# A four-layer graph network on one core: quartered matrix loads in the second pass, a longer planned store, 22 instead of 24 early sums, and a shorter patience beside the LSTM

## The chip, the core and the metric

The kernel runs on one core of one Trainium2 chip. The metric is the device time of one execution in microseconds (us). "About 0.5%" below means a difference of 6.6 us.

## The reference, cut to what matters

There are 32 graphs of 512 nodes with 128 features. `adj` is a symmetric 512 x 512 matrix of zeros and ones with a unit diagonal for each graph. Four layers follow each other, each of the form `x = x + layer(relu(layernorm(x)), adj)`.

```python
# layer 0: masked attention
q, k, v = relu(h Wq + bq), relu(h Wk + bk), relu(h Wv + bv)
x = x + softmax(where(adj, clip(q k^T), -9e15)) v
# layer 1: normalized sums over the neighbours, times the LSTM's output
A = d^-1/2 (adj + I) d^-1/2
lw = lstm(conv(last 128 nodes of h))        # 128 steps in sequence, all 32 graphs at once
x = x + sigmoid((A h) lw)
# layer 2: four chained layers, each with row- and column-normalized sums over adj
# layer 3
x = x + prelu(adj (h W) + bias)
```

The LSTM of layer 1 needs only the last 128 nodes of every graph after layer 0. Its 128 steps depend on each other.

## The kernel before, in words

All work is written as operations of a planner (`Plan`, L522) and is put into a fixed order for each engine when the kernel is built. An operation names its engine (or two that could do it), a cost in us, a rank, and what it reads and writes. The planner places the operation that can start earliest by its own costs, lower ranks first. On the chip every engine then runs its list in that order and waits where the data aren't there yet. So an operation whose data come later than planned holds up everything behind it on its engine.

There are three stages.

* **First pass** (`pass_1`, L1115; ranks from 10,000): for each of the 32 graphs the keys, values and queries, and the attention of the last 128 nodes, then the convolution that feeds the LSTM. Keys, queries' input and values are stored to DRAM (L1156, L1157).
* **LSTM with the second pass beside it** (`lstm`, L1209, ranks 0 to 127; `pass_2`, L1278, ranks from 20,000). A step on TensorE (L1223) is 16 small matmuls in 128 x 32 tiles of the array: 8 for the step itself and 8 that prepare a later one. Then come tanh on ScalarE (L1249, L1261), the cell on VectorE (L1255, L1256), tanh on ScalarE (L1263), and the output with its transpose on VectorE (L1267, L1268), which the next step reads. Between two steps TensorE does work of the second pass: attention of the other 384 nodes (queries L1303, scores L1312, weighted values L1321, all in 128 x 32 tiles), and the sums of layer 1 over the neighbours (`sums_of_1`, L1370, with `aggregate`, L1402; its matmuls are L1406, eight of 128 x 512 on the full array for one graph). The last four graphs' second pass has ranks in the third stage.
* **The rest** (`rest`, L1420, ranks from 30,000): for each graph the product with the LSTM's output, layer 2 and layer 3, in an order of turns that begins with graphs 26 and 27 (`FIRST`).

`EARLY` is the set of graphs whose layer 1 sums are made in the second pass, beside the LSTM: there the whole matrix is loaded (L1291, 1 MB), squared into the form that the sums use while its degrees are accumulated (`squares`, L1355, four ScalarE instructions at L1360), the sums are made, stored (L1348) and loaded again in the third stage. For these graphs layer 1's normalized input overwrites x in place (`place=xc` in `ln_apply`, L1049: L1054 on VectorE, L1057 on ScalarE), so it waits until the store of x to DRAM (L1332) has read it. For other graphs three quarters of each row are enough in the second pass (L1295, 768 KB), and the sums are made in the third stage. Both kinds load the whole matrix in the third stage (L1428), except the two of `FIRST`.

Three planner numbers matter here. `gap` is the time from a transfer's issue slot to its landing, as planned: `LANDED` = 3.8 us for second-pass loads, and 2.0 us by default, which the store at L1332 has. `patience` is by how much an operation may run over the planned start of the next LSTM operation on its engine: 0.15 us for most, `PATIENCE` = 1.3 us for the eight-matmul sums of the second pass, which the planner takes to be 1.86 us long. The rule is in `Plan.run`:

```python
elif held is not None and s < held < s + o.engines[e][0] - o.patience:
    continue
```

SyncE issues nearly all transfers, in the order of its list, and waits at each for what that transfer needs.

Of the kernel before, what the change touches and what calls it, by code (L numbers as in the profile page):

```python
# [13 lines left out]
P = 128  # L14
# [744 lines left out]
def symmetric(ctx, tc, x, adj, weights, cols, rows, lstm_b, prelu_a, out, fail):  # L759
# [12 lines left out]
    nc = tc.nc  # L772
    B, N, D = x.shape
    NT = N // P
    T = P
    L = NT - 1
    NR = N - P
    MANY = 512 // (4 * B)
    LATE = 4
    FIRST = [B - LATE - 2 + k for k in range(2)]  # L780
    EARLY = range(24)
    FOLDS = (4, 7, 10, 13)
    MOVED = range(2, B - 2)
    TURN = 32
    T_STEP = 0.22
    SOON = 9_950.0
    LANDED = 3.8
    PATIENCE = 1.3
    plan_rest = 30_000
    assert D == P and N == 512  # L790

# [14 lines left out]
    def flat(ap):  # L806
        return ap.rearrange("p a b -> p (a b)")

    def f32(ap):
        return ap.bitcast(FP)  # L810
# [5 lines left out]
    def new(tag, shape, name, dtype=FP):  # L816
        return plan.cell(sb, tag, shape, dtype, name)
# [8 lines left out]
    def t_r(n):  # L826
        return max(0.112, n * 0.000455)
# [9 lines left out]
    def t_dma(kb):  # L837
        return 0.1 + kb / 315.0

    def PE(rank, t, fn, r=(), w=(), **k):  # L840
        return plan.op({"PE": (t, fn)}, rank, r, w, **k)

    def ACT(rank, t, fn, r=(), w=(), **k):
        return plan.op({"ACT": (t, fn)}, rank, r, w, **k)
# [7 lines left out]
    def DMA(rank, kb, fn, r=(), w=(), **k):  # L852
        return plan.op({"SP": (max(0.45, t_dma(kb)), fn)}, rank, r, w, gap=k.pop("gap", 2.0), **k)
# [6 lines left out]
    def evict(rank, n, dst, src, r, w, relu=False, scale=None):  # L860

        def act():
            nc.scalar.activation(dst(), src(), AF.Relu if relu else AF.Copy, **({} if scale is None else {"scale": scale}))

        def dve():
            if relu:
                nc.vector.tensor_scalar_max(dst(), src(), 0.0)
            elif scale is not None:
                nc.vector.tensor_scalar_mul(dst(), src(), scale)
            else:  # L870
                nc.vector.tensor_copy(dst(), src())

        slow = 0.0 if scale is None else 0.2
        return plan.op({"ACT": (t_act(n) + slow, act), "DVE": (t_dve(n), dve)}, rank, r, w)
# [157 lines left out]
    def ln_stats(rank, xc, tiles, name, at=0):  # L1032

        st = new("st", (P, NT, 6), f"f_st_{name}")
        mv = new("mv", (P, NT, 2), f"f_mv_{name}")
        for t in tiles:
            DVE(rank, 0.19, lambda t=t: nc.vector.bn_stats(st.t[:, t, :], xc.t[:, t - at, :]), [(xc, t - at)], [(st, t)])
        for t in tiles:
            DVE(rank, 0.09, lambda t=t: nc.vector.bn_aggr(mv.t[:, t, :], st.t[:, t, :]), [(st, t)], [(mv, t)])
        return mv  # L1040
# [8 lines left out]
    def ln_apply(rank, xc, mean, rstd, shift, r, name, relu=False, place=None):  # L1049

        xn = place or new("xn", (P, NT, P), f"f_xn_{name}")
        for t in range(NT):
            def dve(t=t):
                nc.vector.tensor_scalar(xn.t[:, t, :], xc.t[:, t, :], mean(t), rstd(t), OP.subtract, OP.mult)  # L1054

            def act(t=t):
                nc.scalar.activation(xn.t[:, t, :], xc.t[:, t, :], AF.Relu, bias=shift(t), scale=rstd(t))  # L1057
            either = {"ACT": (t_act(P) + 0.13, act)}
            if not relu:
                either["DVE"] = (t_dve(P), dve)  # L1060
            plan.op(either, rank, [(xc, t)] + r, [(xn, t)])
        return xn
# [215 lines left out]
    def pass_2(b):  # L1278
        R = 20_000 + b * 10 if b < B - LATE else 30_000 + (b - B + LATE) * 10 + 15
        dkq, dv, dl, dx = kept[b]  # L1280
        early = b in EARLY
        whole = early or b in FIRST
        a = new("a" if whole else "ar", (P, NT, N if whole else NR), f"f_a_{b}")
# [3 lines left out]
        xc = new("x", (P, NT if whole else L, P), f"f_x2_{b}")  # L1287
        DMA(R, 192, lambda: nc.sync.dma_start(hT.t, dkq.t[:, N:]), [dkq], [hT], gap=LANDED)
        DMA(R, 256, lambda: nc.sync.dma_start(keys.t, dkq.t[:, :N]), [dkq], [keys], gap=LANDED)
        if whole:  # L1290
            DMA(R, 1024, lambda: nc.sync.dma_start(a.t, adj[b].rearrange("(t p) j -> p t j", p=P)), [], [a], gap=LANDED)  # L1291
            ar, deg = squares(R, b, a, "2")
            mask, rows_of = ar, lambda j: f32(ar.t[:, j, :NR])
        else:
            DMA(R, 768, lambda: nc.sync.dma_start(a.t, adj[b, :, :NR].rearrange("(t p) j -> p t j", p=P)), [], [a], gap=LANDED)  # L1295
            mask, rows_of = a, lambda j: a.t[:, j, :]
        DMA(R, 258, lambda: nc.sync.dma_start(v.t, dv.t), [dv], [v], gap=LANDED)
        DMA(R, 192, lambda: nc.sync.dma_start(xc.t[:, :L, :], x[b, :NR].rearrange("(t p) d -> p t d", p=P)), [],
# [30 lines left out]
        if whole and not early:  # L1329
            begun[b] = a, xc, ar, deg  # L1330
        else:
            DMA(R + 5, 192, lambda: nc.sync.dma_start(dx.t, xc.t[:, :L, :]), [(xc, t) for t in range(L)], [dx])  # L1332
        mv = ln_stats(R, xc, range(L), f"r{b}")
        l1 = lns[b]
        POOL(R, 0.15, lambda: nc.gpsimd.tensor_copy(ln1[:, b, 0, :L], mv.t[:, :L, 0]), [mv], [(l1, "mr")])
# [19 lines left out]
    def squares(rank, b, a, name):  # L1355

        ar = new("ar", (P, NT, N), f"f_ar{name}_{b}", FR)
        deg = new("dg", (P, NT), f"f_deg{name}_{b}")
        for t in range(NT):
            ACT(rank, 0.62, lambda t=t: nc.scalar.activation(ar.t[:, t, :], a.t[:, t, :], AF.Square,  # L1360
                                                             accum_out=deg.t[:, t : t + 1]), [a], [(ar, t), (deg, t)])
        return ar, deg

    def diagonal(rank, ar, op):
# [5 lines left out]
    def sums_of_1(rank, b, xc, ar, rs):  # L1370
# [4 lines left out]
        xs = ln_apply(rank, xc, lambda t: ln1[:, b, 0, t : t + 1], lambda t: rs.t[:, t : t + 1], lambda t: sh.t[:, t : t + 1],  # L1375
                      [l1, rs, sh], f"c{b}", place=xc if b in EARLY else None)
        xp = relu_parts(rank, xs, f"c{b}")
        pg = bank(f"f_pg_{b}")
        diagonal(rank, ar, OP.add)
        first = aggregate(rank, xp, ar, pg)  # L1380
        gT = xc if b in EARLY else new("gs", (P, N), f"f_gT_{b}")
        evict(rank, N, lambda: gT.t if b not in EARLY else flat(gT.t), lambda: pg.t, [pg], [gT])
        return gT, first
# [10 lines left out]
    def relu_parts(rank, xs, name):  # L1394

        parts = new("y", (P, NT, 2, P), f"f_xp_{name}", FR)
        ACT(rank, 0.52, lambda: nc.scalar.activation(parts.t[:, :, 0, :], xs.t, AF.Relu), [xs], [(parts, 0)])
        DVE(rank, t_dve(N), lambda: nc.vector.scalar_tensor_tensor(  # L1398
            parts.t[:, :, 1, :], xs.t, 0.0, f32(parts.t[:, :, 0, :]), OP.max, OP.subtract), [xs, (parts, 0)], [(parts, 1)])
        return parts  # L1400

    def aggregate(rank, parts, ar, pg):  # L1402

        def half(k):
            for j in range(NT):
                nc.tensor.matmul(pg.t, parts.t[:, j, k, :], ar.t[:, j, :], start=(k == 0 and j == 0),  # L1406
                                 stop=(k == 1 and j == NT - 1))

        def both():
            half(0)  # L1410
            half(1)
        if rank < plan_rest:
            last = PE(rank, 8 * t_r(N), both, [parts, ar], [pg])
            last.patience = PATIENCE
            return last
        for k in range(2):
            last = PE(rank, 4 * t_r(N), lambda k=k: half(k), [(parts, k), ar], [pg])
        return last

    def rest(b, turn, lw_after):  # L1420
        R = 30_000 + turn * 10
        dkq, dv, dl, dx = kept[b]
        if b in begun:
            a, xc, ar, deg = begun[b]
        else:
            a = new("a", (P, NT, N), f"f_a3_{b}")
            xc = new("x", (P, NT, P), f"f_x3_{b}")
            DMA(R, 1024, lambda: nc.sync.dma_start(a.t, adj[b].rearrange("(t p) j -> p t j", p=P)), [], [a])  # L1428
            DMA(R, 192, lambda: nc.sync.dma_start(xc.t[:, :L, :], dx.t), [dx], [(xc, t) for t in range(L)])
            DMA(R, 64, lambda: nc.sync.dma_start(xc.t[:, L, :], dl.t), [dl], [(xc, L)])  # L1430
            ar, deg = squares(R, b, a, "")
        dinv = new("dv", (P, TURN // NT, NT), f"f_dinv_{b}")
        l1 = lns[b]
        rs = None if b in EARLY else new("rs", (P, NT), f"f_rs_c{b}")

# [12 lines left out]

        if b in EARLY:
            gT, first = new("gs", (P, N), f"f_gT3_{b}"), None  # L1450
# [171 lines left out]
@with_exitstack  # L1622
def kernel(
    ctx: ExitStack,
    tc: tile.TileContext,
    x: bass.AP,
    adj: bass.AP,
    weights: bass.AP,
    cols: bass.AP,
    rows: bass.AP,  # L1630
    lstm_b: bass.AP,
    prelu_a: bass.AP,
    out: bass.AP,
):
    nc = tc.nc
    tensors = (x, adj, weights, cols, rows, lstm_b, prelu_a, out)
    flags = ctx.enter_context(tc.tile_pool(name="flags", bufs=1))
    fail = flags.tile([P, 1], mybir.dt.int32, name="fail")
    with ExitStack() as pools:
        failed = symmetric(pools, tc, *tensors, fail)  # L1640
    with tc.If(failed > 0, preferred_fallthrough_block=False), ExitStack() as pools:
        general(pools, tc, *tensors)
# [58 lines left out]
```

## Time and profile before

| what | value |
|---|---|
| three executions | 1314.0, 1319.26 and 1320.12 us, median 1319.26 |
| profiled execution: time, span | 1317.18 us, 1315.4 us |
| TensorE busy | 1275.1 us (97%) |
| VectorE, ScalarE, GpSimd busy | 992.6 us (75%), 833.2 us (63%), 392.4 us (30%) |
| HBM traffic | 138.16 MB read, 62.65 MB written |
| first LSTM matmul, last one | 184.4 us, 521.4 us from the span's start |

The profiled execution is 2.1 us under the median, and its span lies 1.8 us under its own time. TensorE's busy time counts a matmul until its modelled end, so that neighbours overlap; a stretch at 97% still has room. The program writes each matmul of the 32-bit kind once, and the trace shows it as two records where it is not the one-pass kind: four planned quarter matmuls (called a row below) are eight records.

### The profile page before, as it was taken

How to read it: one execution, taken by the hardware profiler on the slowest of the kernel's cores; microseconds unless marked ns; L12 is line 12 of the kernel's file. 1: busy time of each engine (PE TensorE's matmuls, PEld its weight loads, DVE VectorE, ACT ScalarE, POOL GpSimd, SP SyncE). 2: the span in 40 equal slices, each digit the busy share in tenths (PEclk: the TensorE clock that was granted, in tenths of full speed). 3: DMA queues.
4: the chain of work that ended last, by engine and by line, in shares of the span. 5: the costliest groups of instructions: out<-in, count | busy, mean ns of one | idle time of the engine just before them, and what ended most of it. 6: DMA issues, size and time to landing. Idle time of an engine off the chain costs nothing.

```text
span 1315.4 us, 32850 instructions
## 1 busy us (share of the span) xinstructions
PE 1275.1 (97%) x12097; PEld 974.1 (74%) x12098; DVE 992.6 (75%) x3286; ACT 833.2 (63%) x2095; POOL 392.4 (30%) x737
## 2 busy tenths in 40 slices
PE   8999999999899899999999999999999999999997
PEld 6888866666576666777777878778787787787774
DVE  7998877767788786977676767777676777787654
ACT  5666757667587565577566666666666675676423
POOL 4655532212242222443031322313222132242101
PEclk9999999999999899999999999999999999999999
DMA  8888888766777555999576677777777755673311
GB/s 264 257 277 279 274 272 254 250 214 205 225 243 243 151 165 163 216 213 207 130 158 159 155 156 163 164 158 152 154 164 161 165 120 90 151 170 72 49 33 35
DMA packets 300585, 234.50 MB, mean 178 GB/s; under 512 B 138240, under 2 KB 244480, under 8 KB 300416
## 3 DMA queue, kind: packets, MB, share of 16 engines
q1 hardware_dynamic: 283520, 215.54, 59.4%
q0 software_dynamic: 16896, 16.78, 8.1%
q8 instruction: 97, 1.59, 0.5%
q14 instruction: 72, 0.59, 0.1%
HBM read 138.16 MB, written 62.65 MB: 153 GB/s over the span
## 4 chain that ended last, share of the span: by engine, by line
PE 84%; DVE 6%; DMA 4%; ACT 3%; issue 2%; POOL 1%; SPq 0%; ACTq 0%; DVEq 0%; POOLq 0%
PE f_pa L1406 17%; PE f_py L1510 15%; PE f_pa L1521 14%; PE f_pg L1406 9%; PE f_s L1312 4%; PE f_z L1223 4%; PE f_po L1321 4%; PE f_p L1562 2%; PE f_pol L1173 2%; PE f_pk L1130 2%; PE f_pv L1146 2%; PE f_pl L1464 2%; PE f_sl L1163 2%; DMA f_a<-in_adj_dram 2%; PE f_pd L1198 1%
## 5 line engine op out<-in xcount | busy, mean ns | idle before, releaser
L1406 PE MATMUL f_pa<-f_ar,f_y 128*128 128x512 f32 x1024 | 300.5, 430 | 1.6 <-ACT f_y L1389 1.4
L1406 PEld LDWEIGHTS f_pa<-f_ar,f_y 128*128 128x128 f32 x1024 | 189.4, 188 | 77.9 <-issue 39.9
L1510 PE MATMUL f_py<-f_wf,f_n 128*128 128x128 f32 x1280 | 173.8, 275 | 0.0
L1510 PEld LDWEIGHTS f_py<-f_wf,f_n 128*128 128x128 f32 x1280 | 165.0, 191 | 9.6 <-issue 2.4
L1521 PE MATMUL f_pa<-f_n,f_wf 128*128 128x512 f32 x320 | 153.1, 592 | 0.0
L1525 ACT ACTIVATE f_n<-f_pa,f_bcol 128x512 f32<-128x512 f32 x128 | 88.2, 689 | 92.1 <-PE f_pa L1521 92.1
L1360 ACT ACTIVATE f_ar<-f_a 128x512 fp32r<-128x512 f32 x224 | 138.7, 622 | 6.0 <-DMA f_a<-in_adj_dram 4.6
L1389 ACT CAST f_y<-f_py 128x512 fp32r<-128x512 f32 x128 | 74.8, 585 | 102.3 <-PE f_py L1510 95.3
L1478 POOL DMA_DIRECT2D f_das<-f_ar x32 | 27.0, 842 | 370.5 <-ACT f_ar L1360 309.3
L1312 PE MATMUL f_s<-f_q,f_k 128*32 128x384 f32 x1024 | 106.6, 500 | 6.4 <-issue 5.7
L1321 PE MATMUL f_po<-f_v,f_e 128*32 128x129 f32 x3072 | 108.6, 273 | 4.3 <-issue 4.2
L1321 PEld LDWEIGHTS f_po<-f_v,f_e 128*32 128x32 f32 x3072 | 90.7, 110 | 22.8 <-issue 14.2
L1517 DVE TENSOR_TENSOR f_pa<-f_pa,f_inv 128x512 f32<-128x512 f32 x128 | 86.7, 693 | 26.3 <-PE f_pa L1406 25.8
L1390 DVE TENSOR_TENSOR f_y<-f_py,f_y 128x512 fp32r<-128x512 f32 x128 | 87.4, 684 | 22.2 <-ACT f_y L1389 22.2
L1223 PE MATMUL f_z<-f_w,f_seq 128*32 128x128 f32 x2040 | 87.0, 280 | 13.0 <-DVE f_seq L1268 5.9
L1223 PEld LDWEIGHTS f_z<-f_w,f_seq 128*32 128x32 f32 x2040 | 55.1, 110 | 51.0 <-ACT f_e L1315 12.2
L1521 PEld LDWEIGHTS f_pa<-f_n,f_wf 128*128 128x128 f32 x320 | 57.5, 190 | 44.8 <-issue 36.8
L1483 DVE SCALAR_TENSOR_TENSOR f_junk<-f_a,f_aT 128x1024 bf16<-128x1024 f32 x64 | 78.1, 1221 | 3.0 <-DMA f_aT<-f_das 1.1
L1315 ACT ACTIVATE f_e<-f_s 128x384 f32<-128x384 f32 x128 | 61.5, 484 | 26.0 <-PE f_s L1312 14.1
L1406 PE MATMUL f_pg<-f_ar,f_xp_d 128*128 128x512 f32 x256 | 74.2, 413 | 0.3 <-DVE f_xp_d L1398 0.2
L1085 DVE COPY f_hl_d<-f_n 128x1024 uint16<-128x1024 uint16 x28 | 19.4, 693 | 70.9 <-ACT f_n L1525 70.8
L1510 PE MATMUL f_py<-f_wf,f_T_c 128*128 128x128 f32 x448 | 72.8, 275 | 0.0
(203 smaller groups left out, 2763.8 us busy)
## 6 DMA issues: line engine op xcount, KB each, us to landing
f_a<-in_adj_dram SPq DMA_DIRECT2D x56, 1024.0 KB
f_das<-f_ar POOLq DMA_DIRECT2D x32, 512.0 KB, 4.7
f_dkq<-f_kh SPq DMA_DIRECT2D x32, 448.0 KB
f_dv<-f_v SPq DMA_DIRECT2D x32, 258.0 KB
f_v<-f_dv SPq DMA_DIRECT2D x32, 258.0 KB
f_x<-in_x_dram SPq DMA_DIRECT2D x32, 256.0 KB
f_al<-in_adj_dram SPq DMA_DIRECT2D x32, 256.0 KB
f_k<-f_dkq SPq DMA_DIRECT2D x32, 256.0 KB
```

The lines of the kernel that those rows point to most:

```text
L1223: nc.tensor.matmul(z.t[part, k, :, :], h, w[:, m : m + 4, part], start=False, stop=True, skip_group_check=True)
L1312: PE(R, t_mm(NR), lambda s=s, j=j: quarters(lambda p: nc.tensor.matmul(s.t[p], keys.t[:, j * P + p.start : j * P + p.stop], q.t, start=Tru ...
L1321: PE(R, t_mm(P), lambda t=t, j=j: quarters(lambda p: nc.tensor.matmul(po.t[p, t, :], es[j].t[:, t * P + p.start : t * P + p.stop], v.t[:, ...
L1360: ACT(rank, 0.62, lambda t=t: nc.scalar.activation(ar.t[:, t, :], a.t[:, t, :], AF.Square, accum_out=deg.t[:, t : t + 1]), [a], [(ar, t), ...
L1389: ACT(rank, t_act(N), lambda: nc.scalar.copy(parts.t[:, :, 0, :], src.t), [src], [(parts, 0)])
L1390: DVE(rank, t_dve(N), lambda: nc.vector.tensor_sub(parts.t[:, :, 1, :], src.t, f32(parts.t[:, :, 0, :])), [src, (parts, 0)], [(parts, 1)])
L1406: nc.tensor.matmul(pg.t, parts.t[:, j, k, :], ar.t[:, j, :], start=(k == 0 and j == 0), stop=(k == 1 and j == NT - 1))
L1483: nc.vector.scalar_tensor_tensor(junk, flat(a.t[:, 2 * k : 2 * k + 2, :]), 1.0, flat(aT.t[:, 2 * k : 2 * k + 2, :]), OP.mult, OP.not_equal ...
L1510: nc.tensor.matmul(py.t[:, j, :], nodes[n].t[:, bass.ts(j, P)], wf[:, W_F[i] + c, 0, :], start=False, stop=(c == nch - 1), skip_group_chec ...
L1517: before = DVE(R, t_dve(N), lambda pa=pa: nc.vector.tensor_mul(pa.t, pa.t, inv_row.t), [inv_row], [pa])
L1521: nc.tensor.matmul(pa.t, wf[:, W_F[i] + c, 1, :], nodes[n].t, start=False, stop=(c == nch - 1), skip_group_check=True)
L1525: ACT(R, 0.57, lambda pa=pa, n=n, i=i: nc.scalar.activation(n.t, pa.t, AF.Tanh, bias=bcol[:, i : i + 1]), [pa], [n])
```

## The change

It makes four edits, and no other.

* `EARLY` shrinks from 24 graphs to 22. Graphs 22 and 23 then take the path of graphs 24 and 25: a 768 KB load, no squares, no stored sums in the second pass; the sums in the third stage.
* The matrix of the second pass comes in four transfers of 128 matrix rows each (256 KB, or 192 KB for the shorter rows) instead of one, and each square waits for its own quarter.
* The store of x (L1332) is planned with a gap of `STORED` = 5.0 us instead of 2.0 us.
* `PATIENCE` falls from 1.3 to 0.9 us.

```diff
-    EARLY = range(24)
+    EARLY = range(22)
...
-    PATIENCE = 1.3
+    STORED = 5.0
+    PATIENCE = 0.9
...
         if whole:
-            DMA(R, 1024, lambda: nc.sync.dma_start(a.t, adj[b].rearrange("(t p) j -> p t j", p=P)), [], [a], gap=LANDED)
+            for t in range(NT):
+                DMA(R, 256, lambda t=t: nc.sync.dma_start(a.t[:, t, :], adj[b, t * P : (t + 1) * P, :]), [], [(a, t)], gap=LANDED)
             ar, deg = squares(R, b, a, "2")
...
-            DMA(R, 768, lambda: nc.sync.dma_start(a.t, adj[b, :, :NR].rearrange("(t p) j -> p t j", p=P)), [], [a], gap=LANDED)
+            for t in range(NT):
+                DMA(R, 192, lambda t=t: nc.sync.dma_start(a.t[:, t, :], adj[b, t * P : (t + 1) * P, :NR]), [], [(a, t)], gap=LANDED)
...
-            DMA(R + 5, 192, lambda: nc.sync.dma_start(dx.t, xc.t[:, :L, :]), [(xc, t) for t in range(L)], [dx])
+            DMA(R + 5, 192, lambda: nc.sync.dma_start(dx.t, xc.t[:, :L, :]), [(xc, t) for t in range(L)], [dx], gap=STORED)
...
-                                                             accum_out=deg.t[:, t : t + 1]), [a], [(ar, t), (deg, t)])
+                                                             accum_out=deg.t[:, t : t + 1]), [(a, t)], [(ar, t), (deg, t)])
```

## The prediction

> **What bounds the kernel now.** I read the page first, then the busy times of the three stages, the waits of each engine inside the LSTM's stretch, and last the timeline of single steps.
>
> ```profile
> PE 1275.1 (97%) x12097; PEld 974.1 (74%) x12098; DVE 992.6 (75%) x3286; ACT 833.2 (63%) x2095; POOL 392.4 (30%) x737
> ```
>
> ```profile
> 0.00:184.40 184.40, 179.26 (x1448) 149.30 (x1449) 155.53 (x687) 114.18 (x231) 94.00 (x248) 1.00 0.85 271
> 184.40:521.60 337.20, 313.39 (x6172) 214.03 (x6176) 263.07 (x1081) 229.73 (x813) 86.98 (x162) 0.98 0.67 211
> 521.60:1315.40 793.80, 782.48 (x4489) 610.73 (x4482) 573.97 (x1520) 489.33 (x1051) 211.44 (x328) 1.00 0.65 143
> ```
>
> The columns are the stretch, its length, busy time of TensorE, weight loads, VectorE, ScalarE and GpSimd, the clock, the DMA share and GB/s. TensorE is the bound. In the third stage it is full, and its idle time is the tail (56.19 us busy of the last 66) plus about 1.5 us. So **making the LSTM shorter gains nothing by itself**: matmuls that don't fit beside it are paid after it. Only TensorE time that nobody uses counts, and nearly all that can be had lies in the middle stretch, where 23.8 us are openly idle.
>
> To see the hidden part I price a step from the timeline, start to start. A row of values (L1321) is 0.222 us (72 records in 2.00 us), a row of scores or queries 0.647 us, a graph's eight sums 2.05 us (512.02 to 514.07), a full LSTM step 0.46 us. A step with little beside it repeats after 2.2 us (502.98 to 505.15 is 2.17), which is the way over ScalarE and VectorE. So a step should take the greater of 2.2 us and its fill + 0.46 us, 0.1 us more where full-array work stands between. With the fills read from the built order of the kernel before, the 128 steps come to 305.0 us: fills 230.2, steps 58.9, switches 4.3, idle for the chain 11.6. The stretch took 337.2. So about 32 us are **stalls that the plan didn't foresee**. Which?
>
> ```profile
> ACT f_x L1057 <- DMA f_dx<-f_x: 5.8, 3, 2.1
> ACT f_ar L1360 <- DMA f_a<-in_adj_dram: 2.4, 3, 0.9
> ...
> DVE f_x L1054 <- DMA f_dx<-f_x: 7.1, 5, 2.1
> ...
> PE f_s L1312 <- issue: 5.7, 2, 3.5
> PE f_po L1321 <- issue: 4.2, 4, 3.1
> ```
>
> (Total us, times, longest, inside the LSTM's stretch.) The first three are waits for transfers at the head of in-order lists; the last two, with 1.7 us at L1223, are 11.6 us in which TensorE waits for nothing visible. One case of the first kind:
>
> ```profile
> 351.47 0.32 SPq L1332 DMA_DIRECT2D f_dx<-f_x  x1
> ```
>
> ```profile
> 357.90 0.60 DVE L1054 TENSOR_SCALAR f_x<-f_x,f_ln,f_rs 128x128 f32<-128x128 f32 x2 [1.34 <-DMA f_dx<-f_x]
> 357.98 0.88 ACT L1057 ACTIVATE f_x<-f_x,f_sh_c,f_rs 128x128 f32<-128x128 f32 x2 [2.08 <-DMA f_dx<-f_x]
> ...
> 358.77 0.23 ACT L1249 ACTIVATE f_th<-f_z 128x96 f32<-128x96 f32 x1
> ```
>
> The store is issued at 351.47 and done about 357.9, 6.4 us later; others took 4.5 us (306.61 to 311.1) and 2.9 us (454.09 to 456.95). The plan allows 2.0. Both engines stand before an in-place write, the step's tanh (its matmuls began at 356.62) is queued behind it, and the step takes 3.80 us instead of 2.20.
>
> [...] SyncE's stores here took 2.9 to 6.4 us, beside other traffic, so the measurement decides. [...] eight sums cost 2.05 us between tiled steps and 1.88 when sixteen follow each other (522.16 to 525.93), so the price is near 0.17 us.
>
> **The change, part by part.**
>
> *Store planned with 5.0 us.* Four steps in the stretch carry such a wait: those that begin at 241.3, 310.0, 356.6 and 454.4 run over by 1.87, 1.34, 1.60 and 1.88 us, 6.7 us together. With 5.0 us planned, 2.9 and 4.5 fit and 6.4 does not. I take 5.0 us as gained (bounds 3 to 6.7). The in-place write comes later; behind it are the sums of that graph, which have other graphs' rows to stand in for them. If that cover is missing, it is a step of 2.2 us with less in it, which the order below contains.
>
> *Quartered loads.* The three waits at L1360 in the stretch sum to 2.4 us (0.88, 0.84, 0.70), and one square now waits for a quarter: 1.3 us gained (bounds 0 to 2.4). It costs 3 x 32 = 96 more issues on SyncE's list, 6 fewer from the smaller `EARLY`: 90 x 0.40 us (the median at L1291 is 406 ns) = 36 us. In the stretch SyncE's issues now take 107 of 337 us, so there is room; but the keys, values and stores of other graphs queue behind each quarter. Bounds on that: 0 to +3 us, taken as 0, since the list mostly stands waiting for data.
>
> *22 graphs early, patience 0.9.* These two set the order. In the built order of the changed kernel, TensorE has 20 graphs' sums inside the LSTM instead of 24, 115 rows of scores instead of 120, 28 of queries instead of 29 and 335 of values instead of 331: fills 218.6 instead of 230.2. No step has over 2.4 us of fill (nine had, up to 2.92), yet one pair of steps follows with nothing between. The same formula gives 296.6 us: fills 218.6, steps 58.9, switches 3.9, idle for the chain 15.3. So the LSTM gets 8.4 us shorter and **11.6 us of work go behind it**, where they cost 4 x 1.88 + 6 x 0.647 - 4 x 0.222 = 10.5 us. Net +2.1 us, of which +3.7 is idle for the chain. This is a loss, not a gain: it costs TensorE's time whatever it does for the steps. Bounds: 0 (the filled steps are long in truth, and the new slack absorbs late ScalarE work) to +4.
>
> *One bank marking less.* The order has one L947 matmul fewer inside the LSTM; the step at 316.0 with it ran over by 1.09 us. I take 1.0 us (0 to 1.1).
>
> *ScalarE, VectorE, traffic.* Graphs 22 and 23 drop eight squares (8 x 0.81 us) from the second pass; a diagonal, four normalizations and the split of each move behind the LSTM, where VectorE is busy 574 of 794 us and ScalarE 489: hidden under TensorE. Traffic falls by 2 x (256 + 256 + 256 + 64) KB = 1.7 MB of 234.5, on engines that aren't the bound. The last 176 rows of TensorE's order are the same, so the tail keeps its length.
>
> Sum: +2.1 - 5.0 - 1.3 - 1.0 = **-5.2 us** on 1317.18, so 1312.0; the median shown is 2.1 us above the profiled execution, so **1314** for a median. The LSTM should end near 521.6 - 8.4 - 7.3 = 506 us.
>
> **The rivals.**
>
> *Better than that (1307).* All waits for transfers in the stretch go (6.7 + 2.4), and later writes also free ScalarE on some of the other steps that run over (about 12 us have no named cause; a third is 4). -6 to -7 more. For it: fewer squares and fills without peaks. Against it: the other overruns may be waits of another kind.
>
> *The stalls only move (1320).* A new order has new misjudged arrivals, so the 32 us stay, with the +2.1 and the marking's -1.0. For it: stores varied from 2.9 to 6.4 us, one constant doesn't cover them. Against: the plan errs less.
>
> *Slower (1327): the third stage starts before its matrices are there.* The LSTM ends some 16 us earlier, but the bytes of the first turns must come by the same queue: in 550 to 600 us DMA is already busy 0.87. A turn reloads 1 MB, 5.1 us at the 206 GB/s of that stretch, and writes and reads half of that for the transpose. If TensorE then waits for about three matrices, that adds 13 us and the case decides from a wait of about 12 us. Against: TensorE's only wait there was 1.2 us at 600 us, and SyncE's list is planned anew.
>
> **Numbers.** My case 50%, own range 1309 to 1319; better 22%; moved stalls 13%; slower 15%. About 0.5% (6.6 us) is what a measurement of this kernel can tell from no change. Faster by more, under 1312.7: the better case and a third of mine, 0.38. Slower by more, over 1325.9: most of the last and a little of the third, 0.15. Within: 0.47. The range is 1304 to 1326: it takes in the better case with 3 us of its spread and ends at the lower half of the slow one.
>
> **What would show it.** Right: waits for f_dx at L1054 and L1057 under 2 us each in the stretch, those at L1360 under 1 us; last L1223 near 506 us; TensorE full after it, and about 10 us more between the LSTM's end and the span's. Wrong: an LSTM that ends after 515 us (stalls moved), or waits of TensorE between 505 and 620 us (third stage starved). The issue waits are 11.6 us here by chance of where they fall; half or twice of that would shift the result by 6 to 10 us with no part in the change.

## The result, and the profile after

The changed kernel takes **1309.43 us** (median of seven executions, 1305.65 to 1314.59) against 1319.26 us (median of seven, 1314.0 to 1323.4): ratio 0.994, interval 0.9913 to 0.9966. It is faster by 0.6%, a little more than the 0.4% that was forecast, and lies at the lower edge of the prediction's own range (1309 to 1319).

The profiled execution of the changed kernel took 1314.59 us, with a span of 1312.7 us. It is the slowest of the seven, 5.2 us over their median, so the two traces differ by 2.6 us where the medians differ by 9.8. So below the traces say where time lies, and the ratios say how much there is.

First the page's busy times of the changed kernel, then its second and third stage (columns as before: stretch, length, TensorE, weight loads, VectorE, ScalarE, GpSimd, clock, DMA share, GB/s).

```profile
PE 1272.8 (97%) x12097; PEld 979.3 (75%) x12097; DVE 988.7 (75%) x3274; ACT 834.8 (64%) x2093; POOL 393.3 (30%) x733
```

```profile
183.70:499.90 316.20, 298.46 (x6127) 211.26 (x6131) 255.04 (x1071) 221.94 (x791) 83.66 (x158) 0.99 0.71 223
499.90:1312.70 812.80, 794.75 (x4534) 618.80 (x4525) 575.85 (x1513) 498.68 (x1073) 216.16 (x329) 0.99 0.63 138
```

The totals hardly move; the stages do. The LSTM is 21 us shorter and ends at 499.9 us, and the third stage is 19 us longer. That is the trade that the prediction described, at larger amounts: it had the LSTM end at 506 us and about 10 us more behind it.

TensorE's waits inside the LSTM's stretch of the changed kernel (total us, times, longest):

```profile
PE f_po L1324 <- issue: 7.4, 5, 3.7
PE f_z L1224 <- DVE f_seq L1269: 4.3, 11, 1.8
```

In the same stretch neither VectorE nor ScalarE has a wait for a store of x or for a matrix any more: of the three transfer rows that the prediction shows, nothing is left. What is left are the waits named "issue": 8.7 us, against 11.6. Now TensorE's longest wait between the LSTM's end and 620 us:

```profile
PE f_xt_c L859 <- ACT f_xn_c L1058: 3.7, 1, 3.7
```

In the first 60 us after the LSTM TensorE is idle for 5.5 us; before the change it was 0.9 us. The timeline shows that wait from both ends, VectorE first (start, duration, then the idle time before it and what ended it):

```profile
522.95 1.23 DVE L1486 SCALAR_TENSOR_TENSOR f_junk<-f_a,f_aT 128x1024 bf16<-128x1024 f32 x1 [3.35 <-DMA f_aT<-f_das]
```

```profile
530.50 1.10 PE L859 MATMUL f_xt_c<-f_ident,f_xn_c 128*128 128x128 f32 x3 [3.73 <-ACT f_xn_c L1058]
```

VectorE stands 3.35 us at the head of its list for a transposed matrix. The statistics that it makes behind this go over GpSimd to a normalization on ScalarE, and TensorE meanwhile has nothing for 3.73 us. This is the mechanism of the slower rival, at a part of its price.

### The profile page after: what moved, and what is told of

The parts are those of the page before. It is cut to its first block, busy times and chain, and to the rows that moved or that the text cites. A ratio compares the mean times of both kernels' runs of the same rounds, so it can differ in the third digit from the quotient of the medians.

```text
span 1312.7 us, 32944 instructions
## 1 busy us (share of the span) xinstructions
PE 1272.8 (97%) x12097; PEld 979.3 (75%) x12097; DVE 988.7 (75%) x3274; ACT 834.8 (64%) x2093; POOL 393.3 (30%) x733
## 4 chain that ended last, share of the span: by engine, by line
PE 85%; DVE 5%; ACT 3%; POOL 2%; DMA 2%; issue 2%; SPq 0%; ACTq 0%; DVEq 0%; POOLq 0%
PE f_pa L1409 17%; PE f_pa L1524 14%; PE f_py L1513 14%; PE f_pg L1409 9%; PE f_po L1324 5%; PE f_s L1315 5%; PE f_z L1224 4%; PE f_p L1565 2%; PE f_pol L1174 2%; PE f_pk L1131 2%; PE f_pv L1147 2%; PE f_pl L1467 2%; PE f_sl L1164 2%; PE f_pd L1199 1%; PE f_pq L1306 1%
## 5 line engine op out<-in xcount | busy, mean ns | idle before, releaser
L1409 PE MATMUL f_pa<-f_ar,f_y 128*128 128x512 f32 x1024 | 295.0, 426 | 2.1 <-ACT f_y L1392 2.1
L1528 ACT ACTIVATE f_n<-f_pa,f_bcol 128x512 f32<-128x512 f32 x128 | 88.2, 689 | 93.6 <-PE f_pa L1524 93.4
L1363 ACT ACTIVATE f_ar<-f_a 128x512 fp32r<-128x512 f32 x216 | 133.7, 622 | 7.1 <-DMA f_a<-in_adj_dram 3.7
L1324 PE MATMUL f_po<-f_v,f_e 128*32 128x129 f32 x3072 | 107.0, 274 | 7.5 <-issue 7.4
L1324 PEld LDWEIGHTS f_po<-f_v,f_e 128*32 128x32 f32 x3072 | 90.4, 110 | 21.8 <-issue 15.2
L1315 PE MATMUL f_s<-f_q,f_k 128*32 128x384 f32 x1024 | 103.3, 490 | 0.6 <-issue 0.6
L1486 DVE SCALAR_TENSOR_TENSOR f_junk<-f_a,f_aT 128x1024 bf16<-128x1024 f32 x64 | 78.1, 1220 | 5.7 <-DMA f_aT<-f_das 4.7
L1058 ACT ACTIVATE f_xn_c<-f_x,f_sh_c,f_rs_c 128x128 f32<-128x128 f32 x138 | 58.0, 486 | 24.2 <-DVE f_sh_c L1066 24.1
```

What stands on the lines that cost most here:

```text
L1315: PE(R, t_mm(NR), lambda s=s, j=j: quarters(lambda p: nc.tensor.matmul(s.t[p], keys.t[:, j * P + p.start : j * P + p.stop], q.t, start=Tru ...
L1324: PE(R, t_mm(P), lambda t=t, j=j: quarters(lambda p: nc.tensor.matmul(po.t[p, t, :], es[j].t[:, t * P + p.start : t * P + p.stop], v.t[:, ...
L1486: nc.vector.scalar_tensor_tensor(junk, flat(a.t[:, 2 * k : 2 * k + 2, :]), 1.0, flat(aT.t[:, 2 * k : 2 * k + 2, :]), OP.mult, OP.not_equal ...
L1528: ACT(R, 0.57, lambda pa=pa, n=n, i=i: nc.scalar.activation(n.t, pa.t, AF.Tanh, bias=bcol[:, i : i + 1]), [pa], [n])
```

## The experiments

Twelve kernels were run, in three groups, each group beside the kernel before on the same chip. In the kernel before, 59 executions of the first group spread from 1306.6 to 1327.0 us, so single executions say little and the ratios carry the verdicts. Each group ran on another chip; where kernels of two groups are compared in us below, the difference of their ratios agrees within 2 us. Shifts of a line or three against the kernel before come from the added lines.

| kernel | edits it has | median us | ratio to before (95%) |
|---|---|---|---|
| the change | all | 1309.43 | 0.994 (0.9913 to 0.9966) |
| quarters_same_order | four transfers, before's order | 1309.76 | 0.9941 (0.9918 to 0.9965) |
| quarters_only | four transfers, own order | 1311.93 | 0.9967 (0.9947 to 0.9986) |
| stored_only | store planned with 5.0 | 1336.8 | 1.0139 (1.0099 to 1.0179) |
| order_pair | 22 early, patience 0.9 | 1322.44 | 1.0032 (1.0013 to 1.0051) |
| stored_quarters | four transfers, store 5.0 | 1318.1 | 0.9999 (0.9974 to 1.0023) |
| after_single | all but four transfers | 1331.59 | 1.0108 (1.0081 to 1.0136) |
| after_stored2 | all but store 5.0 | 1320.94 | 1.0037 (1.0021 to 1.0053) |
| after_e24 | all but 22 early (24) | 1316.81 | 0.9999 (0.998 to 1.0018) |
| after_e20 | all, 20 early | 1322.3 | 1.0036 (1.0022 to 1.0049) |
| after_p13 | all but patience 0.9 (1.3) | 1310.7 | 0.9947 (0.9929 to 0.9965) |
| after_turn8 | all, transpose planned with 8.0 | 1312.33 | 0.9958 (0.994 to 0.9976) |
| store_elsewhere | before's order, early stores send other bytes | 1312.93 | 0.997 (0.9949 to 0.999) |

The next table takes the profiled executions apart: the length of the LSTM's stretch, what the prediction's formula gives for the built order, the rest of the stretch (stalls), the TensorE work placed between the steps (fill), the length of what follows the LSTM, and how much that is over the kernel before once the fill that moved is added back (post + fill - 1023.8). Each row is one execution.

| kernel | LSTM | formula | stalls | fill | post | lost after the LSTM |
|---|---|---|---|---|---|---|
| before | 337.4 | 305.0 | 32.4 | 230.2 | 793.6 | 0 |
| the change | 316.3 | 296.6 | 19.6 | 218.6 | 812.7 | 7.5 |
| quarters_same_order | 324.6 | 305.0 | 19.6 | 230.2 | 798.2 | 4.6 |
| store_elsewhere | 326.7 | 305.0 | 21.7 | 230.2 | 797.8 | 4.2 |
| stored_only | 336.4 | 303.5 | 32.9 | 222.5 | 811.7 | 10.4 |
| quarters_only | 318.5 | 303.0 | 15.6 | 222.1 | 810.3 | 8.6 |
| order_pair | 322.7 | 297.4 | 25.3 | 213.8 | 815.5 | 5.5 |
| stored_quarters | 317.0 | 298.4 | 18.6 | 218.7 | 812.5 | 7.4 |
| after_single | 326.1 | 298.0 | 28.1 | 215.6 | 822.5 | 14.3 |
| after_stored2 | 313.4 | 296.6 | 16.9 | 211.0 | 819.5 | 6.7 |
| after_e24 | 321.9 | 297.0 | 24.9 | 216.8 | 817.9 | 10.9 |
| after_e20 | 315.4 | 295.5 | 19.9 | 215.4 | 823.7 | 15.3 |
| after_p13 | 321.9 | 298.7 | 23.2 | 221.6 | 806.7 | 4.5 |
| after_turn8 | 312.9 | 296.6 | 16.3 | 218.6 | 811.4 | 6.2 |

The change and after_turn8 have the same order inside the LSTM and differ by 3.4 us there: single executions scatter by at least that much.

### The matrix in four transfers

**Four transfers in the order of before.** One planned operation issues all four, so every compute engine's list is that of the kernel before. Only the 1 MB loads are split; the six of 768 KB stay whole.

```diff
-            DMA(R, 1024, lambda: nc.sync.dma_start(a.t, adj[b].rearrange("(t p) j -> p t j", p=P)), [], [a], gap=LANDED)
+            DMA(R, 1024, lambda: [nc.sync.dma_start(a.t[:, t, :], adj[b, t * P : (t + 1) * P, :]) for t in range(NT)], [], [a], gap=LANDED)
```

> The kernel before with every instruction of TensorE, ScalarE, VectorE and GpSimd in the same order, but each 1 MB load of the second pass's matrix is issued as four transfers in a row at the same place of SyncE's list. If the four transfers themselves make the chip's stalls smaller (a square waits for its quarter alone), the LSTM gets 3 to 10 us shorter and the time 1 to 4 us below before. If the gain of 4 us that quarters alone had came from the order that the planner made of them, within 1.5 us of before.

Measured: 1309.76 us, ratio 0.9941 (six executions). This one edit gives as much as the whole change, and more than the 1 to 4 us that were expected of it. Its stages:

```profile
182.50:507.10 324.60, 306.13 (x6180) 210.18 (x6184) 262.06 (x1082) 228.91 (x811) 89.03 (x162) 1.00 0.70 219
507.10:1305.30 798.20, 783.29 (x4481) 611.60 (x4474) 573.93 (x1519) 489.38 (x1051) 212.06 (x328) 0.99 0.65 142
```

TensorE's work in the LSTM is that of the kernel before, in a stretch that is 12.8 us shorter, and the clock is 1.00 there where it was 0.98. Waits in that stretch, of VectorE, ScalarE and TensorE:

```profile
DVE f_x L1054 <- DMA f_dx<-f_x: 9.9, 6, 3.3
```

```profile
ACT f_x L1057 <- DMA f_dx<-f_x: 5.8, 2, 3.3
```

```profile
PE f_s L1312 <- issue: 1.7, 1, 1.7
PE f_pq L1303 <- issue: 0.5, 1, 0.5
```

The waits for the store are all still there (9.9 and 5.8 us; 7.1 and 5.8 before). The waits for the matrix, 2.4 us, are gone. What the prediction didn't count on is the third thing: the "issue" waits of TensorE fell from 11.6 to 2.7 us. The kernel before shows what such a wait looks like. First TensorE, then SyncE's list some microseconds earlier:

```profile
425.72 0.48 PE L1312 MATMUL f_s<-f_q,f_k 128*32 128x384 f32 x1
429.71 0.86 PE L1312 MATMUL f_s<-f_q,f_k 128*32 128x384 f32 x4 [3.51 <-issue]
```

```profile
419.95 0.42 SPq L1291 DMA_DIRECT2D f_a<-in_adj_dram  x1
```

A row of scores begins, and its next matmul comes 3.51 us later although the profile names nothing that it waits for (the last section comes back to this). A 1 MB load was issued 6.3 us ahead of it. The other stall of this size, 3.07 us before 332.05, follows the 1 MB load issued at 323.93 by 5 us. And with each comes a clock of half (kernel before, columns as in the table of stages; the clock is the third number from the end):

```profile
426.20:428.90 2.70, 0.00 (x1) 0.00 (x0) 1.24 (x6) 0.00 (x0) 0.00 (x0) 0.99 0.82 258
428.90:435.70 6.80, 5.99 (x60) 3.63 (x64) 2.26 (x11) 2.25 (x8) 1.77 (x4) 0.50 0.05 18
```

```profile
333.30:336.70 3.40, 3.40 (x37) 1.87 (x34) 2.52 (x14) 1.04 (x4) 0.00 (x0) 0.50 0.33 124
```

TensorE is busy for 9.4 us at half clock in these two windows. A single score matmul (L1312) took 0.85 us there, at 431.20, and 0.48 us at 425.72 above. If all of it runs at half its speed (that pair gives 0.56), an estimated 4.7 us of the 9.4 are lost. With four transfers the same places read, in the same order of work:

```profile
326.00:340.00 14.00, 13.16 (x267) 8.94 (x270) 12.20 (x54) 9.03 (x34) 4.20 (x9) 1.00 0.93 301
405.00:440.00 35.00, 32.80 (x728) 22.72 (x723) 29.99 (x129) 24.66 (x87) 10.95 (x20) 1.00 0.66 203
```

So the gain of 12.8 us in the LSTM is about 8.9 of issue waits, an estimated 4.7 of half clock and 2.4 of matrix waits, less 2.8 that VectorE waits longer for the store; that makes 13.2. (One execution of each; store_elsewhere, which also keeps the order and its 1 MB loads, has 8.6 us of issue waits and one window of half clock of 3.4 us, so a part of this fall can be scatter.) The third stage gives 4.6 us back: TensorE idles 3.5 us in its first 60 instead of 0.9, and has one window of half clock (3.4 us from 541.2).

**Four transfers with an order of their own.** The two loads and the squares of the change, added to the kernel before.

```diff
+            for t in range(NT):
+                DMA(R, 256, lambda t=t: nc.sync.dma_start(a.t[:, t, :], adj[b, t * P : (t + 1) * P, :]), [], [(a, t)], gap=LANDED)
...
-            [a], [(ar, t), (deg, t)])
+            [(a, t)], [(ar, t), (deg, t)])
```

> The kernel before with the second pass's matrix in four transfers, nothing else. Theory A: the waits of ScalarE for f_a inside the LSTM (2.4 us) fall under 0.5 us, the waits for f_dx stay near 6 us, the time 1 to 2 us below before. Theory B: within 1 us of before, or 1 to 3 us above, for 96 more transfers on SyncE's list. Theory C: anything within 5 us.

Measured: 1311.93 us, ratio 0.9967. The LSTM is still shorter (318.5 us), and the issue waits are 4.1 us; but the planner, which now sees four issues, builds an order with 8.1 us less fill and 6.3 us more idle for the chain, and 8.6 us are lost after the LSTM instead of 4.6. By the medians the order takes back 2.2 us of what the transfers give, which the two intervals do not tell from nothing.

**The change without four transfers.**

```diff
-            for t in range(NT):
-                DMA(R, 256, lambda t=t: nc.sync.dma_start(a.t[:, t, :], adj[b, t * P : (t + 1) * P, :]), [], [(a, t)], gap=LANDED)
+            DMA(R, 1024, lambda: nc.sync.dma_start(a.t, adj[b].rearrange("(t p) j -> p t j", p=P)), [], [a], gap=LANDED)
```

> The changed kernel with the matrix in one transfer again. Order: fill 215.6 us inside the LSTM, formula 298.0, idle for the chain 19.8 us. If the quarters are what the planned store needs to pay (alone it lost 19 us, with quarters nothing), 8 us or more above the changed kernel, with waits of ScalarE for f_a of 2 us or more inside the LSTM. By the arithmetic of the prediction, 2 to 4 us above it.

Measured: 1331.59 us, ratio 1.0108: 22 us slower than the change. TensorE's waits in the LSTM:

```profile
PE f_po L1322 <- issue: 12.6, 8, 3.6
PE f_z L1224 <- DVE f_seq L1269: 7.4, 16, 1.7
PE f_s L1313 <- issue: 4.3, 3, 1.9
PE f_z L1224 <- issue: 3.1, 3, 1.3
```

The three issue rows are 20.0 us, against 8.7 in the change. ScalarE's waits for the matrix, of which 2 us or more were expected, are only 0.7 us, and the clock in this LSTM is 1.00.

Five pairs of kernels differ in their edits by the transfers alone (four of them then also in the order that the planner builds), and in each the issue waits are fewer with four of them: 11.6 and 2.7 (the same order), 11.6 and 4.1 (quarters_only), stored_only 12.2 and stored_quarters 8.0, after_single 20.0 and the change 8.7, order_pair 11.5 and after_stored2 6.0. In the last pair the time does not follow (ratios 1.0032 and 1.0037). Nor do four transfers remove these waits: over all kernels they come to 2.7 to 11.7 us with four (after_e24 has 11.7) and 8.5 to 20.0 with one, and the change itself still has one of 3.7 us, which begins at 330.14 behind four quarters issued in a row from 325.09 (TensorE's row L1324 above).

### The store of x

**Its wait taken away, the order kept.** For the graphs with early sums the store sends bytes of a weight tile, so the in-place write has nothing to wait for and all else stays; x of these graphs isn't stored.

```diff
-            DMA(R + 5, 192, lambda: nc.sync.dma_start(dx.t, xc.t[:, :L, :]), [(xc, t) for t in range(L)], [dx])
+            DMA(R + 5, 192, lambda: nc.sync.dma_start(dx.t, w[:, :W_CONV, :] if early else xc.t[:, :L, :]), [(xc, t) for t in range(L)], [dx])
```

> The kernel before with the same instructions in the same order on every engine, but for the early graphs the store at L1332 takes its 192 KB from a tile of weights that nothing overwrites, so that nothing waits for it; x as loaded back in the third stage is therefore not the graph's (the part left out). This takes the wait away and leaves traffic, order and plan. Theory A: the four steps that ran over by 6.7 us go back to about 2.2 us, and since the LSTM's end moves by as much with the same work behind it, the time falls by 5 to 7 us (0.4 to 0.5%). Theory B and C: within 1.5 us of before.

Measured: 1312.93 us, ratio 0.997 (0.9949 to 0.999), that is 4 to 5 us, with an interval from 1 to 7. The waits for the store are gone. In the profiled execution the LSTM is 10.7 us shorter and the third stage gives 4.2 us back, as above. The 6.7 us that the prediction counted can't be read off it singly: this execution also had 3.1 us less of issue waits (8.5 instead of 11.6), 1.7 less of matrix waits and an estimated 3 less lost at half clock, 14.5 us together. The median agrees with the 5.0 us that the prediction took.

**The store planned with 5.0, and nothing else.**

```diff
+    STORED = 5.0
...
-            DMA(R + 5, 192, lambda: nc.sync.dma_start(dx.t, xc.t[:, :L, :]), [(xc, t) for t in range(L)], [dx])
+            DMA(R + 5, 192, lambda: nc.sync.dma_start(dx.t, xc.t[:, :L, :]), [(xc, t) for t in range(L)], [dx], gap=STORED)
```

> The kernel before with the store of x planned at 5.0 us, nothing else. Theory A (the waits for the store held up LSTM steps): no wait for f_dx of over 1 us inside the LSTM, the LSTM shorter by about 5 us, the time 5 us (0.4%) below before. Theory B (the gain comes from the order that 22 early graphs and the shorter patience make): within 1 us of before. Theory C (any new order lands somewhere within 5 us by chance): no tie between the waits gone and the time.

Measured: 1336.8 us, ratio 1.0139, the slowest of all. The waits for the store fall to 0.5 and 1.0 us, as planned. The longest wait of ScalarE for a transfer and waits of TensorE in this kernel's LSTM, then TensorE's between 519 and 600 us:

```profile
ACT f_ar L1361 <- DMA f_a<-in_adj_dram: 4.2, 2, 2.8
```

```profile
PE f_po L1322 <- issue: 6.5, 6, 2.4
PE f_bT L1014 <- DMA f_rowb<-in_rows_dram: 4.1, 1, 4.1
PE f_z L1224 <- ACT f_ar L1361: 4.0, 2, 2.0
```

```profile
PE f_xt_c L859 <- ACT f_xn_c L1058: 5.0, 1, 5.0
```

Here the third rival, "the stalls only move", came true: 32.4 us of stalls before and 32.9 now (one execution of each), with the squares waiting for the matrix and a row of biases waited for in place of the store. The new order also has 7.7 us less fill in an LSTM of almost the same length, and after it 10.4 us are lost: 5.9 more idle in the first 60 us, and 6.8 us at half clock from 548.8.

**The store and the four transfers.** The two edits above together.

> The kernel before with the planned store of 5.0 us and the four transfers together; 24 early graphs and patience 1.3 as before. Its built order has 218.7 us of fill inside the LSTM and a formula of 298.4 us. Theory A (stalls gone count, and the order is a small cost): LSTM about 16 us shorter, 10 us of work behind it, the time 5 to 8 us below before. Theory D (from the first runs: the planned store alone cost 19 us because the order lost fill inside the LSTM without shortening it, and waited at the start of the third stage; each edit's effect depends on the order that all of them give): 3 us below to 6 above before.

Measured: 1318.1 us, ratio 0.9999. The four transfers are worth 18.7 us on top of the planned store, and 4 to 8 us without it (quarters_only and quarters_same_order).

**The change with the store planned at 2.0.**

```diff
-    STORED = 5.0
+    STORED = 2.0
```

> The changed kernel with the store of x planned at 2.0 us again. Order: fill 211.0, formula 296.6, idle for the chain 22.5 us. By the prediction's step (5 us of stalls avoided by the planned store) 5 us above the changed kernel, with waits for f_dx of 4 us or more inside the LSTM. If the planned store is worth nothing once the loads come in quarters, within 2 us of it.

Measured: 1320.94 us, ratio 1.0037; 11.5 us slower than the change. The waits that return, on ScalarE and VectorE, are about half of those in the kernel before (5.8 and 7.1):

```profile
ACT f_x L1058 <- DMA f_dx<-f_x: 2.6, 4, 1.6
```

```profile
DVE f_x L1055 <- DMA f_dx<-f_x: 3.7, 4, 1.9
```

The LSTM of this profiled execution is even 2.9 us shorter than the change's. It has 7.6 us less fill and 7.2 us more idle for the chain, and pays the fill behind. So in this company the 5.0 us seem to be worth more by the order that they make than by the waits that they remove. That is not shown: the trace pair differs by only 3.0 of the 11.5 us, and the rest stays unassigned.

### The number of early sums and the patience

**These two alone.**

```diff
-    EARLY = range(24)
+    EARLY = range(22)
...
-    PATIENCE = 1.3
+    PATIENCE = 0.9
```

> The kernel before with 22 early graphs and patience 0.9, single loads, store planned at 2.0 us. Theory A: the LSTM is about 8 us shorter, but that work returns behind it; waits for f_dx stay; the time 2 us above before (0 to 4). Theory B: the time 5 to 9 us below before. Theory C: anything within 5 us.

Measured: 1322.44 us, ratio 1.0032: a loss of 4.2 us, where the prediction's steps for order and marking made +1.1 (+2.1 and -1.0). It is no test of that sum, though: without the other edits these two build another order. It has 16.4 us less fill than the kernel before (213.8) in an LSTM that the formula makes 7.6 us shorter (297.4), which by the prediction's own arithmetic is a loss of about 8 us, not 2.1.

**The change with 24, and with 20.**

```diff
-    EARLY = range(22)
+    EARLY = range(24)
```

> The changed kernel with 24 early graphs again. Order: fill 216.8 us inside the LSTM, idle for the chain 17.5 us against 15.3. By the arithmetic of the prediction 2 us above the changed kernel, that is 1311 to 1313 where that is 1310. If the smaller number of early graphs is what makes the change pay, 6 us or more above it.

```diff
-    EARLY = range(22)
+    EARLY = range(20)
```

> The changed kernel with 20 early graphs. Order: fill 215.4 us, formula 295.5, idle for the chain 17.6 us. If fewer early graphs pay in themselves (24 to 22 was worth 7 us here), another 3 to 7 us below the changed kernel. If what counts is the idle for the chain and the start of the third stage, within 3 us of it.

Measured: 0.9999 with 24, 0.994 with 22, 1.0036 with 20. There is no trend in it; the fill of 24 (216.8) is even below that of 22. With 20 the LSTM is as short as the change's, and the third stage begins badly: TensorE has a wait of 7.6 us, and beside it this window of half clock (columns of the stages):

```profile
528.90:539.10 10.20, 4.29 (x12) 3.52 (x13) 6.24 (x12) 2.34 (x5) 0.00 (x0) 0.50 0.81 184
```

**The change with the old patience.**

```diff
-    PATIENCE = 0.9
+    PATIENCE = 1.3
```

> The changed kernel with the patience of 1.3 us again. Order: fill 221.6 us, idle for the chain 14.3 us against 15.3, three steps over 2.4 us of fill. By the arithmetic 1 us below the changed kernel (0 to 2): a shorter patience shortens the LSTM and buys no TensorE time. If steps held up by sums are what costs, 4 us or more above it.

Measured: 1310.7 us, ratio 0.9947. The patience makes no difference that can be measured. The profiled LSTM is 5.6 us longer and the rest 6.0 us shorter, 3.0 us of it fill that moved and the rest 3.6 more of stalls against 3.0 less lost behind. That agrees with the rule that the prediction began with: a shorter LSTM by itself gains nothing.

### The start of the third stage

**The transpose planned with 8.0 us.** If the wait of VectorE at L1486 costs the 3.73 us of TensorE, then a plan that expects the transpose later should put other work first.

```diff
-        plan.op({"SP": (3.0, lambda: nc.sync.dma_start_transpose(out=aT.t, in_=das.t))}, R + 2, [das], [aT], gap=4.0)
+        plan.op({"SP": (3.0, lambda: nc.sync.dma_start_transpose(out=aT.t, in_=das.t))}, R + 2, [das], [aT], gap=8.0)
```

> The changed kernel with the landing of the matrix's transpose (L1483) planned at 8.0 us instead of 4.0, so that the symmetry check at L1486 stands later in VectorE's list. The order inside the LSTM is the same. If the waits at the start of the third stage (6.6 us of TensorE in the profiled execution, the longest 3.7 us behind a check that waited 3.35 us for its transpose) are a lasting cost, 3 to 6 us below the changed kernel, and no wait for f_aT over 1 us between 500 and 560 us. If they come and go from execution to execution, within 2 us of it.

Measured: 1312.33 us, ratio 0.9958; no better than the change. VectorE's wait for the transpose is gone from the trace, but TensorE still idles 4.1 us in the first 60 us after the LSTM instead of 5.5, and its longest wait there is 3.6 us, now for a tanh on ScalarE (L1528). The loss there isn't one wait that one number removes.

## Why the prediction was right, step by step

The direction, the size (1314 us against 1309.43) and the trade between the stages were right. The working behind them was right in parts, and that its sum came out near is partly luck: of the two gains in it, the one priced at 5.0 us (the planned store) loses 18 to 19 us when it stands alone, and the one priced at 1.3 us (the four transfers) gains 4 to 8.

**Where TensorE's time counts.** Right as far as it was tried: after_p13 has 5.6 us more of LSTM and 6.0 us less behind it, at the same time. Work in the third stage wasn't as safe as "full" said, though; see the rivals.

**Order, +2.1 us, and the marking, -1.0.** Together +1.1. The 0.17 us for eight sums between tiled steps is the difference of two measured times, 2.05 and 1.88 us. For the 0.1 us of a step behind full-array work the trace of the kernel before has 0.13: on its chain the 16 matmuls of a step take 0.57 us behind such work (at 223.45, 225.62 and 229.11) and 0.44 us behind tiled work (215.85 and 218.28). What makes these differences is not shown. The move was as forecast in direction: in the change the LSTM is shorter and the third stage longer, by more than the 8.4 and 10.5 us of this step. The step itself was not measured singly: the two edits alone cost 4.2 us, in an order for which the same arithmetic gives about 8, and within the change going back to 24 graphs costs 7 us. The price depends on the rest of the order, and no single number holds. Not in the sum was what an order loses after the LSTM, 7.5 us in the change.

**Store, -5.0 us (3 to 6.7).** The price of the wait agrees with the measurement (4 to 5 us with the order kept, interval 1 to 7). That the longer plan would deliver it was not: alone it costs 18 to 19 us. In the change the waits are gone, and taking the 5.0 back costs 11.5 us, probably more by the order than by the waits.

**Quartered loads, -1.3 us (0 to 2.4): the term that was mis-sized.** It measured -6.9 us on the same order by the medians of the group (1316.66 to 1309.76), -22 us inside the change, and nothing beside the order pair alone. Its bound above was drawn around the visible waits for the matrix, 2.4 us. The issue waits, 11.6 us, and the half clock behind them were set aside as "chance of where they fall", with "no part in the change". On the same order they had the largest part, and with four transfers instead of one they fell in all five pairs. The table of stages did show a clock of 0.98 in the LSTM against 1.00 in the stage after, which was one sign of them.

**The sum of the trace pair.** LSTM 21.1 us shorter: 8.4 by the formula, 12.8 by stalls (the prediction: 8.4 and 7.3). The stalls' part is near what can be named: 6.7 for the store, 2.4 for the matrix, 1.1 for the marking, 2.9 for issue waits and an estimated 1.3 for less half clock (10.2 us to 6.8) make 14.4. After the LSTM 19.1 us more: 10.5 moved, 4.6 idle at its start, up to 1.7 from a window of half clock at 531.7; 2.3 have no name.

**The rivals.** Better: its sign, no transfer waits left in the LSTM, is what the trace shows, and the median lies nearer to its 1307 than to 1314; a good part was given back later. Stalls move: wrong for the change (32.4 to 19.6), right for stored_only. Slower: TensorE does wait at the start of the third stage, 4.6 us more and some half clock. It was priced at 13 us and decides from 12, and the change stays under that; after_e20 and after_single lose 15.3 and 14.3 us after the LSTM and are slower than before. Even the two kernels that keep the order of before lose 4 to 5 us there when the LSTM ends 12 to 15 us earlier. Why isn't shown: in quarters_same_order SyncE's issues just behind the LSTM come about 14.5 us earlier too, as much as its end does (14.7), and only those from 580 us of the kernel before on have fallen back to 11.

**What the edits add up to.** Alone they measure +1.39, -0.33 and +0.32%, together +1.38% if they added; the change is -0.6%. Laid out by edit, eight of the kernels make a full table (ratio to before; the intervals are 0.1 to 0.4% to each side):

| | one transfer | four transfers |
|---|---|---|
| 24 early, patience 1.3, store 2.0 | 1 (before) | 0.9967 |
| 24 early, patience 1.3, store 5.0 | 1.0139 | 0.9999 |
| 22 early, patience 0.9, store 2.0 | 1.0032 | 1.0037 |
| 22 early, patience 0.9, store 5.0 | 1.0108 | 0.994 (the change) |

Four transfers gain 0.3 to 1.7% in three rows and nothing in the third. The store planned with 5.0 loses in three of its four comparisons and gains only in the change, by 1.0%. The order pair loses in two and gains in two. Each edit of a planner's number makes another order, and orders that look alike by the formula (295.5 to 298.7 us) lose from 4.5 to 15.3 us after the LSTM.

**Open.** In the traces of the kernel before and of the change an issue wait ends 1.2 to 1.6 us after a packet of one queue (last section); what ties these waits to the 1 MB loads is not isolated. No cause was found for what each order loses after the LSTM. No version was clearly better than the change; quarters_same_order, with one edit of its four, has the same ratio, and the two were not run against each other.

## What to carry to other kernels

When an engine that bounds the time waits for nothing visible, look at which large transfers run beside it, and try the same bytes in smaller transfers with everything else kept: here such waits were 11.6 us with 1 MB transfers and 2.7 us with 256 KB. A clock below one in one stage can point there but need not: after_single has 20.0 us of such waits at a clock of 1.00. Where a planner makes the order, price an edit of its numbers by an experiment that keeps the order (other bytes, several transfers in one planned slot) before trusting one that rebuilds it: here the same wait was worth -0.3% removed in place and +1.4% planned away, alone. What is won ahead of a full stage is checked at that stage's start: 4 to 15 us were lost there in these kernels.

## What the runs showed of the hardware that was not expected

**One 1 MB transfer against four of 256 KB.** Same bytes, same queue (215.54 MB on q1 in both traces), same order of work on the compute engines: issue waits of TensorE in the LSTM 11.6 and 2.7 us, time 0.6% apart. The page of the kernel before has a queue that it calls instruction, with the number of packets, MB and share:

```profile
q8 instruction: 97, 1.59, 0.5%
```

That is 16.4 KB for each, one for about 253 of TensorE's 24,533 recorded instructions. The packets' own times in the traces tell more of the issue waits. The LSTM of the kernel before has 49 of these packets, one in about 7 us, and seven issue waits; that of the change has eight issue waits. Each of the fifteen, of 0.2 to 3.7 us, ends 1.2 to 1.6 us after a packet of this queue has ended. The four longest of the kernel before (3.51, 3.07, 2.16 and 1.69 us) end 1.41, 1.30, 1.42 and 1.43 us after one. By this timing TensorE seems to stand there until what the packet brings has come; that is a reading of the times, and no view names it. The four packets took 0.92 to 0.99 us, the median of all is 1.04; they start late. Counted by the instructions that TensorE has begun, against a straight line through the 49 packets, these four start 132 to 152 instructions late, and no other of the 49 more than 104. In the change the packets ahead of its two longest waits (3.70 and 2.35 us) start 149 and 153 late, and no other more than 82. What makes them start late is not isolated. quarters_same_order has 97 packets too, so it isn't that fewer come. In the kernel before 42 of the 49 have no issue wait behind them, and the waits behind the other seven come to 11.6 of 337 us.

**The clock after a short stall.** TensorE's granted clock is 0.50 for 3.4 us (333.3 to 336.7) and 6.8 us (428.9 to 435.7) in the LSTM of the kernel before, and for 10.2 us (528.9 to 539.1) in after_e20. In the kernel before 3.07 us of idle was followed by the 3.4 us at half clock, and the 6.8 us began at 428.9, inside the 3.51 us of idle that end at 429.71. If half of the work time behind them is lost, these two stalls cost an estimated 4.8 us (3.07 and half of 3.40) and 6.5 us (3.51 and half of 5.99). But the length of one stall does not tell whether the half clock follows. In the change a shorter one is followed, from 354.2 on, by 3.4 us of it; in after_single one of 3.56 us is followed by none, and the next 3.5 us run at 1.00:

```profile
353.32 0.64 PE L1224 MATMUL f_z<-f_w,f_seq 128*32 128x128 f32 x16 [1.82 <-DVE f_seq L1269]
354.20:357.60 3.40, 3.40 (x16) 2.22 (x18) 2.64 (x9) 2.19 (x7) 1.43 (x2) 0.51 0.90 291
```

```profile
200.30 0.98 PE L1322 MATMUL f_po<-f_v,f_e 128*32 128x129 f32 x27 [3.56 <-issue]
200.30:203.80 3.50, 3.36 (x100) 2.69 (x103) 1.64 (x7) 1.53 (x6) 0.00 (x0) 1.00 0.95 295
```
